# A five-layer decoder step on one core: another order and queue for the first loads of the scan, the first sines of cross attention behind the last scan, its output weights in eight pieces

## The chip, the core and the metric

The kernel runs on one core of one Trainium2 chip. A core has TensorE (PE: matmuls; PEld is its weight load), VectorE (DVE), ScalarE (ACT), GpSimd (POOL) and SyncE (SP). Loads and stores are issued from SP's and ACT's queues (and a few indirect ones from POOL's) and are moved by the core's 16 DMA engines. The metric is the device time of one execution in microseconds (us), as the median of several runs.

## The reference

Input `x` is 16 sequences of 128 tokens with 512 features. Two decoder layers follow one another; after each block the input is added and a layernorm taken. What matters here are the first two blocks.

The first is a state-space scan. For each token, `dt = softplus(x Wdt + b)` (512 values) and `B`, `C` (16 values each) come from products with `x`. With 16 states per feature the recurrence over the 128 tokens is

```
h = exp(dt * A) * h + (dt * x) * B
y = sum over the 16 states of h * C
```

and `y` goes through an output product with a bias.

The second is cross attention. Queries (16 heads of 128) come from `x`, keys and values (4 heads of 128) from 128 context tokens and the 128 tokens of `x`. Queries and keys are divided by their root mean square, weighted, and turned by rotary angles `position * inv_freq`, which needs the sine and cosine of 64 angles per token. Softmax over 256 keys, the values, and an output product (2048 by 512) follow. The rest (a ternary feed-forward, causal attention, a second cross attention, and a mixture of experts) is not touched.

## The kernel before, in words

Five stages run one after another. The work is cut into 16 blocks of 128 tokens, one per sequence.

The scan (`stage_ssm`) takes two blocks at a time and 16 states for each pair: 128 units. For a unit u, ACT forms the decays (`decays`, four exponentials), POOL the products `dBx` (`terms`), DVE runs the recurrence (`scan`), DVE or POOL multiplies by `C`, and PE adds the result into PSUM by transposes (`add`). SP loads `B` and `C` of unit u+4 (`widths_in`); POOL forms `dBx` of u+2. Between the units, PE also computes keys and values of the context for both attention blocks (`keys_values`), which are stored to DRAM. In this loop each instruction is pinned to the order in which the program writes it. `dBx` has four rooms, the copies `y` and `yT` of the output have three.

Ahead of the loop stand the first loads: the projection weights `xpw` and the first `xT` on SP, the step weights `dtw` (1 MB) on ACT, biases (`xpb`, three copies each of `dtb` and `outb`), `A_log`, and the weights `wk`, `wv` of the second cross attention (2 MB) on SP, then two context blocks. POOL makes each bias row into three bf16 parts (lines 156 to 164), then forms the four step sums (`step_sum`).

After the loop, a layernorm of the first two blocks, the last transposes, and the output product of the last pair (`output`, `output_sum`) close the stage. Then `load_output_weights` asks for the 4 MB of cross attention's output weights in two loads, into rooms of a pool of five: the rooms come free when the products that read them are done.

Cross attention (`stage_xattn`) loads the norm weights, positions and frequencies, forms with `SinTables` the sines and cosines of a group of four blocks (some 20 DVE instructions and two ACT ones), and multiplies them by the norm weights on POOL (`tables`). `project` then makes keys and queries of a block in steps: a load of the context's keys (`raw`), products on PE, the rotary step on DVE (`rope`), transposes on PE. Attention itself runs as a pipeline of 128 units, with `project` of the next block beside it. `clear_rows` issues some 100 DRAM clears of 388 KB for a later stage from SP's queue, one per step. Outside the scan's loop a scheduler orders each engine's instructions by its own estimate of when they become ready; `keep_in_program_order` holds one behind what is already written for its engine.

A tile's room is reused in turn: an instruction that writes a tile waits for the readers of the tile that had the room before.

Of the kernel before, what the change touches and what calls it, by code (L numbers as in the profile page):

```python
# [107 lines left out]
def stage_ssm(k):  # L108
# [9 lines left out]
    with ExitStack() as ctx:  # L118
# [20 lines left out]
        def load_x(p):  # L139
            xT = wk.tile([P, KC, TQ], F32, tag="xT", name="xT", bufs=1)  # L140
            nc.sync.dma_start(xT, a["xT"][:, p * TQ : (p + 1) * TQ].rearrange("(c p) t -> p c t", p=P))
            return xT

        nc.sync.dma_start(xpw, a["xpwT"].rearrange("(c p) e -> p c e", p=P))
        xT0 = load_x(0)
        nc.scalar.dma_start(dtw, a["dtwT"].rearrange("(c p) e -> p c e", p=P))
        nc.sync.dma_start(xpb, a["xpb"].unsqueeze(1))
        wholes = []
        for i, n in enumerate(("dtb", "outb")):
            whole = wk.tile([65, D], F32, tag="BC", name="whole", bufs=6)  # L150
            nc.gpsimd.memset(whole, 0.0)
            for r in (0, 32, 64):
                nc.sync.dma_start(whole[r : r + 1], a[n].unsqueeze(0))
            wholes.append(whole)
        nc.sync.dma_start(alog, a["A_log"].rearrange("(c p) n -> p c n", p=P))
# [16 lines left out]
        for i, n in enumerate(("wk", "wv")):  # L172
            nc.sync.dma_start(kvw[:, i], a["x2_" + n + "T"].rearrange("(c p) e -> p c e", p=P))
# [55 lines left out]
        def sums_out(st, i):  # L229
            y = wk.tile([P, KC, P], F32, tag="y", name="yT", bufs=3)  # L230
            q.nc.scalar.copy(y, st.py[i])
            st.yT[i] = y
# [6 lines left out]
        def turned_out(st, i):  # L239
            y = st.y[i] = wk.tile([P, KC, P], F32, tag="y", name="y", bufs=3)  # L240
            q.nc.scalar.copy(y, st.pt[i])
# [72 lines left out]
        def terms(u):  # L314
            st, n = units[u]
            dBx = st.dBx[n] = wk.tile([P, KC, TQ], F32, tag="dBx", name="dBx", bufs=4)
# [43 lines left out]
        nc.scalar.dma_start(outw, a["outwT"].rearrange("(c p) e -> p c e", p=P))  # L360
# [8 lines left out]
        for u, (st, n) in enumerate(units):  # L369
# [9 lines left out]
            if u >= 6:  # L379
                next(pieces, None)  # L380
            if n in (8, 9):
                i = n - 8
                q.nc.sync.dma_start(k.x[p * BQ + i], a["x"][p * BQ + i])
# [52 lines left out]
        q.nc.vector = nc.vector  # L436
        layernorm(k, k.x[0:2], k.x[0:2], keep=tc.keep_in_program_order)
        q.nc = nc
        if kv.out:
            keys_values_out()  # L440
# [9 lines left out]
    load_output_weights(k)  # L450


class SinTables:
# [4 lines left out]
    def __init__(self, k, pool, wk):  # L458
        nc, a = k.nc, k.args
        self.k, self.wk = k, wk  # L460
        pos = pool.tile([P, 2, NB], I32, name="pos")
        nc.sync.dma_start(pos, a["posT"].rearrange("s p b -> p s b"))
        self.invf = pool.tile([P, self.HF], F32, name="invf")
        nc.sync.dma_start(self.invf, a["inv_freq"].partition_broadcast(P))
        self.posf = pool.tile([P, 2, NB], F32, name="posf")
        nc.vector.tensor_copy(self.posf, pos)

    def group(self, g):
        nc, wk, HF, BG = self.k.nc, self.wk, self.HF, self.BG
# [7 lines left out]
        ang = wk.tile([P, N], F32, tag="m1", name="ang", bufs=4)  # L477
        r = wk.tile([P, N], F32, tag="m2", name="ang_r")
        sin = wk.tile([P, 2, BG, HF], F32, tag="sin", name="sin", bufs=1)
        cos = wk.tile([P, 2, BG, HF], F32, tag="cos", name="cos", bufs=1)  # L480
        for s in range(2):
            nc.vector.tensor_tensor(
# [3 lines left out]
            )  # L486
        for turns in (4096.0, 1.0):
            nc.vector.tensor_scalar(r, ang, 1.0 / (2 * PI * turns), MAGIC, ALU.mult, ALU.add)
            nc.vector.tensor_scalar(r, r, MAGIC, None, ALU.subtract)
            for c in parts:  # L490
                nc.vector.scalar_tensor_tensor(ang, r, -c * turns, ang, ALU.mult, ALU.add)
        lim = 3.1415925
        nc.vector.tensor_scalar(r, ang, lim, -lim, ALU.min, ALU.max)
        nc.scalar.activation(sin.rearrange("p s b f -> p (s b f)"), r, AF.Sin)

        r = wk.tile([P, N], F32, tag="m2", name="ang_r2")
        nc.vector.tensor_scalar(ang, ang, PI / 2, None, ALU.add)
        nc.vector.tensor_scalar(r, ang, PI, -2 * PI, ALU.is_gt, ALU.mult)
        nc.vector.tensor_tensor(r, r, ang, ALU.add)
        nc.vector.tensor_scalar(r, r, lim, -lim, ALU.min, ALU.max)  # L500
# [34 lines left out]
def load_output_weights(k):  # L535
    nc, a = k.nc, k.args
    k.wo = [k.wslot().rearrange("p (h e) -> p h e", h=8) for _ in range(2)]
    for i in range(2):
        nc.sync.dma_start(k.wo[i], a["xa_woT"][i * 1024 : (i + 1) * 1024].rearrange("(h p) e -> p h e", p=P))
# [20 lines left out]
def stage_xattn(k):  # L560
# [9 lines left out]
    with ExitStack() as ctx:  # L570
# [8 lines left out]
        w2 = []  # L579
        for name in ("q_norm_w", "k_norm_w"):  # L580
            w = cst.tile([P, HD], F32, name=f"w_{name}")
            nc.sync.dma_start(w, a[name].partition_broadcast(P))
            ws = cst.tile([P, HD], F32, name=f"ws_{name}")
            nc.vector.tensor_scalar(ws[:, 0:64], w[:, 64:128], -1.0, None, ALU.mult)
            nc.vector.tensor_copy(ws[:, 64:128], w[:, 0:64])
            w2.append((w, ws))
        sincos = SinTables(k, cst, wk)
        trig = {}
# [32 lines left out]
        def angles(g):  # L621
            trig[g] = sincos.group(g)
            yield

        def norm_inputs(p):
            xs = k.x[2 * p : 2 * p + 2]
            layernorm(k, xs, xs)
# [168 lines left out]
        running = [clear_rows(k, cst)]  # L796
# [1255 lines left out]
```

## Time and profile before

| what | value |
|---|---|
| runs | 3062.74, 3057.76, 3058.74 us |
| median | 3058.74 us |
| the profiled execution | 3050.86 us, span 3049.1 us |
| mean granted clock of TensorE | 0.991 |
| PE busy | 2925.1 us (96%) |
| DVE, ACT, POOL busy | 1891.8, 1355.2, 1491.1 us |
| first scan begins | 32.46 us |
| last scan ends | 507.2 us |
| first roped query turned on PE | 560.79 us |

A row of the timeline has start and duration in us, the engine, the line in the kernel, the operation, what it writes and reads, its shapes, and in brackets how long the engine was idle before it and what ended that. Several equal instructions are merged (x8). A row of SPq or ACTq is the issue of a transfer, not the transfer. Line 66 stands for every pinned instruction, so those are told apart by their tiles. The median of the runs lies 7.9 us above the profiled execution.

### The profile page before, as it was taken

How to read it: one execution, taken by the hardware profiler on the slowest of the kernel's cores; microseconds unless marked ns; L12 is line 12 of the kernel's file. 1: busy time of each engine (PE TensorE's matmuls, PEld its weight loads, DVE VectorE, ACT ScalarE, POOL GpSimd, SP SyncE). 2: the span in 40 equal slices, each digit the busy share in tenths (PEclk: the TensorE clock that was granted, in tenths of full speed). 3: DMA queues.
4: the chain of work that ended last, by engine and by line, in shares of the span. 5: the costliest groups of instructions: out<-in, count | busy, mean ns of one | idle time of the engine just before them, and what ended most of it. 6: DMA issues, size and time to landing. Idle time of an engine off the chain costs nothing.

```text
span 3049.1 us, 40643 instructions
## 1 busy us (share of the span) xinstructions
PE 2925.1 (96%) x13720; PEld 1832.3 (60%) x13744; DVE 1891.8 (62%) x4221; ACT 1355.2 (44%) x3315; POOL 1491.1 (49%) x1274
## 2 busy tenths in 40 slices
PE   7999999799999999999999989999999999999998
PEld 6666665455555555555787656666566666666665
DVE  5989997766666666655898797666643322242224
ACT  5777775333333343336444797655533322222221
POOL 7999995433333433331333574246535553333331
PEclk9999999899999999999999999999999999999999
DMA  6654444780000000004100200134356665554541
GB/s 189 205 140 123 125 128 140 251 290 11 11 8 11 11 8 15 8 26 149 35 1 1 70 1 2 60 110 163 126 188 236 225 226 168 164 192 165 163 149 60
DMA packets 170978, 331.59 MB, mean 109 GB/s; under 512 B 21966, under 2 KB 79822, under 8 KB 169228
## 3 DMA queue, kind: packets, MB, share of 16 engines
q1 hardware_dynamic: 127948, 222.01, 23.6%
q0 software_dynamic: 19200, 64.18, 6.2%
q10 hardware_dynamic: 23616, 42.74, 3.7%
q8 instruction: 111, 1.82, 0.2%
q14 instruction: 103, 0.84, 0.1%
HBM read 244.57 MB, written 137.43 MB: 125 GB/s over the span
## 4 chain that ended last, share of the span: by engine, by line
PE 67%; DVE 13%; ACT 2%; POOL 2%; issue 1%; DMA 1%; SPq 0%; ACTq 0%; DVEq 0%; POOLq 0%
PE y L1799 8%; PE pu L1782 7%; PE pg L1782 7%; PE pq L645 7%; PE po L765 6%; PE po L977 4%; PE ao L754 3%; PE sc L714 2%; PE pkv L66 2%; PE pt L508 2%; PE pg L957 2%; PE pw L1451 2%; PE pu L957 2%; PE ptx L508 1%; PE ps L1366 1%
## 5 line engine op out<-in xcount | busy, mean ns | idle before, releaser
L734 POOL TENSOR_TENSOR pr<-pr,sm 128x512 f32<-128x512 f32 x128 | 135.4, 1058 | 352.7 <-DVE sm L733 274.1
L66 POOL TENSOR_TENSOR dBx<-dtx,BC 128x1024 f32<-128x1024 f32 x126 | 298.4, 2390 | 0.6
L1782 PE MATMUL pg<-gu,xgT 128*128 128x352 f32 x784 | 296.5, 460 | 1.4 <-ACT act L1785 1.4
L1782 PE MATMUL pu<-gu,xgT 128*128 128x352 f32 x784 | 296.1, 459 | 0.0
L727 ACT ACTIVATE pr<-sc,mx,sf 128x256 f32<-128x256 f32 x256 | 142.2, 560 | 324.5 <-DVE mx L720 262.5
L1786 DVE SCALAR_TENSOR_TENSOR act<-pu,row,act 128x352 f32<-128x352 f32 x98 | 57.1, 582 | 358.2 <-PE pu L1782 353.1
L1799 PE MATMUL y<-dn,aT 128*128 128x512 f32 x588 | 268.4, 593 | 0.0
L1827 POOL TENSOR_TENSOR x<-got,x 128x512 f32<-128x512 f32 x120 | 151.6, 1269 | 222.3 <-DMA got<-results,gidx 221.8
L66 ACT ACTIVATE h<-dt,negA 128x254 f32<-128x254 f32 x508 | 242.2, 477 | 16.9
L765 PE MATMUL po<-w,aT 128*128 128x512 f32 x512 | 234.8, 597 | 2.5 <-DVE aT L759 2.5
L645 PE MATMUL pq<-w,xT 128*128 128x512 f32 x512 | 232.2, 596 | 1.3 <-ACT v L680 0.7
L1820 POOL DMA_INDIRECT got<-results,gidx x120 | 115.8, 965 | 230.7 <-DMA results<-yo 170.6
L66 DVE TENSOR_TENSOR_SCAN h<-h,dBx 128x1024 f32<-128x1024 f32 x80 | 183.2, 2290 | 34.4 <-ACT h L66 24.8
L1782 PEld LDWEIGHTS pu<-gu,xgT 128*128 128x128 f32 x784 | 149.0, 190 | 82.6 <-DVE act L1786 0.2
L1785 ACT ACTIVATE act<-pg 128x352 f32<-128x352 f32 x98 | 45.5, 464 | 304.3 <-PE pg L1782 269.4
L1782 PEld LDWEIGHTS pg<-gu,xgT 128*128 128x128 f32 x784 | 141.4, 190 | 64.7 <-ACT act L1785 1.9
L616 POOL TENSOR_TENSOR m<-m,m 128x512 f32<-128x512 f32 x96 | 121.4, 1265 | 111.8 <-DVE m L611 111.6
L66 PE MATMUL pkv<-w,cT 128*128 128x512 f32 x384 | 171.5, 593 | 1.1 <-ACT y L66 1.1
L1811 DVE COPY yo<-y 128x512 f32<-128x512 f32 x90 | 62.2, 691 | 165.6 <-PE y L1799 148.3
L1799 PEld LDWEIGHTS y<-dn,aT 128*128 128x128 f32 x588 | 104.2, 190 | 100.7 <-issue 94.1
L1774 ACT COPY xgT<-ptx 128x512 f32<-128x512 f32 x98 | 57.4, 586 | 234.5 <-PE ptx L508 228.9
L967 POOL TENSOR_TENSOR lo<-sg,hi 128x512 fp32r<-128x512 f32 x64 | 84.2, 1317 | 153.8 <-ACT hi L966 153.7
(402 smaller groups left out, 6770.3 us busy)
## 6 DMA issues: line engine op xcount, KB each, us to landing
bucket<-zeros SPq DMA_DIRECT2D x96, 388.0 KB, 8.0
row<-bucket SPq DMA_DIRECT2D x90, 388.0 KB, 3.7
BC<-bcd SPq DMA_DIRECT2D x128, 256.0 KB, 5.2
results<-yo ACTq DMA_DIRECT2D x90, 256.0 KB, 3.4
gu<-in_moe_guT SPq DMA_DIRECT2D x16, 1408.0 KB, 7.9
x_k<-kv ACTq DMA_DIRECT2D x32, 256.0 KB, 3.8
x_v<-kv ACTq DMA_DIRECT2D x32, 256.0 KB, 5.3
v<-x_v SPq DMA_DIRECT2D x32, 256.0 KB, 2.7
```

Of the source, the lines that this page charges most:

```text
L66: return self.tc.keep_in_program_order(call(*args, **kw))
L616: nc.gpsimd.tensor_tensor(m1, m1, m2, ALU.add)
L645: nc.tensor.matmul(ps, src[:, c], w[c], start=c == 0, stop=c == KC - 1)
L727: nc.scalar.activation(pr[:, j], st.sc[g, i][:, j], AF.Exp, scale=st.sf[:, h : h + 1], bias=st.mx[g, i][:, j : j + 1], accum_out=sm[:, j : ...
L734: nc.gpsimd.tensor_tensor(pr, pr, sm.unsqueeze(2).to_broadcast([P, 2, 2 * P]), ALU.mult)
L765: nc.tensor.matmul(st.po, aT[:, j], k.wo[h // 8][:, h % 8], start=h == 0, stop=h == G * J - 1)
L957: nc.tensor.matmul(p[:, e], w[:, c, at : at + P], sn.qT[:, :, c], start=c == 0, stop=c == KC - 1)
L977: nc.tensor.matmul(sn.po[i], part[:, e, i * P : (i + 1) * P], k.fd[hc // 8][:, hc % 8], start=hc == 0 and part is parts[0], stop=hc == 15 ...
L1782: nc.tensor.matmul(ps, u.xT[:, c], gu[:, c, lo : lo + I], start=c == 0, stop=c == KC - 1)
L1799: self.nc.tensor.matmul(u.y, u.aT[:, c], u.w[1][:, c], start=c == 0, stop=c == 2)
L1820: nc.gpsimd.indirect_dma_start(out=got[:, :], out_offset=None, in_=k.results[h][g][0:end, :], in_offset=bass.IndirectOffsetOnAxis(ap=self. ...
L1827: nc.gpsimd.tensor_tensor(k.x[b], got, k.x[b], ALU.add)
```

## The change

Four things change.

First, the loads at the start. The order on SP is written out and kept: `xpw`, `xT`, the three copies of `dtb`, `xpb`, `A_log`, and `outb` last (the scheduler puts the two context blocks ahead of `outb`). `dtw` comes in two halves on ACT. `wk` and `wv` move from SP's queue to ACT's, and the scan's output weights `outw` are kept behind the first keys on ACT.

Second, rooms: `dBx` has three instead of four, `y` and `yT` two instead of three. A new pool `head` holds the norm weights, positions and first sine tables through both stages.

Third, the head of cross attention. The four small loads are issued at unit 30 of the scan (`Head`), and the first group of angles is formed after the last scan, in two rooms of the tag `hs` that the scan no longer needs. These DVE instructions are kept in program order behind the layernorm, which is itself kept now; the same holds for the layernorms of later input blocks (`norm_inputs`).

Fourth, the output weights come in eight pieces of 512 KB, issued one per step of attention beginning with the third; the scheduler puts five of them ahead of the first `raw`.

```diff
-        xT0 = load_x(0)
-        nc.scalar.dma_start(dtw, a["dtwT"].rearrange("(c p) e -> p c e", p=P))
-        nc.sync.dma_start(xpb, a["xpb"].unsqueeze(1))
...
+        wholes = [wk.tile([65, D], F32, tag="BC", name="whole", bufs=6) for _ in range(2)]
+        def load_row(i):
+            for r in (0, 32, 64):
+                keep(nc.sync.dma_start(wholes[i][r : r + 1], a[("dtb", "outb")[i]].unsqueeze(0)))
+        for whole in wholes:
             nc.gpsimd.memset(whole, 0.0)
...
+        keep(nc.sync.dma_start(xT0, a["xT"][:, 0:TQ].rearrange("(c p) t -> p c t", p=P)))
+        load_row(0)
+        keep(nc.sync.dma_start(xpb, a["xpb"].unsqueeze(1)))
+        keep(nc.sync.dma_start(alog, a["A_log"].rearrange("(c p) n -> p c n", p=P)))
+        load_row(1)
+        for h in range(2):
+            es = slice(2 * h * P, (2 * h + 2) * P)
+            nc.scalar.dma_start(dtw[:, :, es], a["dtwT"][:, es].rearrange("(c p) e -> p c e", p=P))
...
-            nc.sync.dma_start(kvw[:, i], a["x2_" + n + "T"].rearrange("(c p) e -> p c e", p=P))
+            keep(nc.scalar.dma_start(kvw[:, i], a["x2_" + n + "T"].rearrange("(c p) e -> p c e", p=P)))
...
-            y = wk.tile([P, KC, P], F32, tag="y", name="yT", bufs=3)
+            y = wk.tile([P, KC, P], F32, tag="y", name="yT", bufs=2)
...
-            dBx = st.dBx[n] = wk.tile([P, KC, TQ], F32, tag="dBx", name="dBx", bufs=4)
+            dBx = st.dBx[n] = wk.tile([P, KC, TQ], F32, tag="dBx", name="dBx", bufs=3)
...
-        nc.scalar.dma_start(outw, a["outwT"].rearrange("(c p) e -> p c e", p=P))
+        keep(nc.scalar.dma_start(outw, a["outwT"].rearrange("(c p) e -> p c e", p=P)))
...
+            if u == 30:
+                k.head = Head(k, q.nc.sync)
...
-        q.nc.vector = nc.vector
-        layernorm(k, k.x[0:2], k.x[0:2], keep=tc.keep_in_program_order)
         q.nc = nc
+        layernorm(k, k.x[0:2], k.x[0:2], keep=keep)
+        room = [wk.tile([P, KC, TQ], F32, tag="hs", name="room") for _ in range(2)]
+        k.head.fill(keep)
+        k.head.trig = k.head.sines.group(
+            0, lambda what: {"ang": room[0][:, 0:2], "ang_r": room[1][:, 0:2], "ang_r2": room[1][:, 2:4]}[what]
+            .rearrange("p c t -> p (c t)") if what in ("ang", "ang_r", "ang_r2") else k.head.out[what], keep,
+        )
...
-    load_output_weights(k)
+class Head:
+    HD = 128
+    def __init__(self, k, sync):
+        a, pool = k.args, k.head_pool
+        self.k, self.raw, self.w2 = k, [], []
+        for name in ("q_norm_w", "k_norm_w"):
+            w = pool.tile([P, self.HD], F32, name=f"w_{name}")
+            sync.dma_start(w, a[name].partition_broadcast(P))
+            self.w2.append((w, pool.tile([P, self.HD], F32, name=f"ws_{name}")))
+        self.sines = SinTables(k, pool, sync)
+        self.out = {n: pool.tile([P, 2, SinTables.BG, SinTables.HF], F32, name=f"{n}0") for n in ("sin", "cos")}
+    def fill(self, keep):
+        vector = self.k.nc.vector
+        for w, ws in self.w2:
+            keep(vector.tensor_scalar(ws[:, 0:64], w[:, 64:128], -1.0, None, ALU.mult))
+            keep(vector.tensor_copy(ws[:, 64:128], w[:, 0:64]))
+        keep(vector.tensor_copy(self.sines.posf, self.sines.pos))
...
-def load_output_weights(k):
+def output_weights(k):
     nc, a = k.nc, k.args
     k.wo = [k.wslot().rearrange("p (h e) -> p h e", h=8) for _ in range(2)]
-    for i in range(2):
-        nc.sync.dma_start(k.wo[i], a["xa_woT"][i * 1024 : (i + 1) * 1024].rearrange("(h p) e -> p h e", p=P))
+    yield
+    yield
+    for n in range(8):
+        hs = slice(2 * (n % 4), 2 * (n % 4) + 2)
+        nc.sync.dma_start(k.wo[n // 4][:, hs], a["xa_woT"][n * 256 : (n + 1) * 256].rearrange("(h p) e -> p h e", p=P))
+        yield
...
-            layernorm(k, xs, xs)
+            layernorm(k, xs, xs, keep=tc.keep_in_program_order)
...
-        running = [clear_rows(k, cst)]
+        running = [output_weights(k), clear_rows(k, cst)]
...
-            if t == -12 or r == 0 and b > 0 and b < NB and b % 4 == 0:
-                running.append(angles(max(b, 0) // 4))
+            if r == 0 and b > 0 and b < NB and b % 4 == 0:
+                running.append(angles(b // 4))
```

The instructions of the first sines are the same 20 or so as before; the tables of the later groups stay where they were.

## The prediction

> **What bounds the kernel now.** I read the page's slices first, then the busy time by stretch, the waits, and the rows in order of time at the two places that the change touches.
>
> ```profile
> PE   7999999799999999999999989999999999999998
> POOL 7999995433333433331333574246535553333331
> ```
>
> A slice is 76.2 us. TensorE is full nearly everywhere, so a gain must be found where it is not: slice 0 (the start) and slice 7 (533 to 610, the way from the scan into cross attention). POOL is full through the scan. The busy time by stretch around slice 7 (PE, PEld, DVE, ACT, POOL, then clock and DMA):
>
> ```profile
> 508.00:527.00 19.00, 17.11 (x61) 8.64 (x60) 11.40 (x54) 3.97 (x7) 0.19 (x1) 1.00 0.37 137
> 527.00:541.00 14.00, 10.54 (x24) 4.10 (x22) 4.66 (x15) 3.45 (x5) 0.00 (x0) 1.00 0.75 239
> 541.00:560.00 19.00, 5.84 (x15) 3.13 (x16) 13.16 (x34) 1.39 (x3) 11.22 (x15) 0.55 0.96 317
> 560.00:600.00 40.00, 37.55 (x131) 20.24 (x130) 28.67 (x73) 16.29 (x38) 19.30 (x21) 1.00 0.81 280
> ```
>
> From 541 to 560 PE works 5.8 of 19 us, at a mean clock of 0.55, while VectorE is at 13.2. The waits from 500 to 600 (us, times, longest):
>
> ```profile
> POOL tk0s L595 <- ACT sin L494: 20.0, 1, 20.0
> PE pt L508 <- POOL m L677: 17.5, 4, 15.7
> DVE ws_q_norm_w L584 <- DMA raw<-x_k: 9.4, 1, 9.4
> ```
>
> One PE wait is 15.7 us; its cause is two steps back. The rows in order of time:
>
> ```profile
> 505.05 21.25 SPq L539 DMA_DIRECT2D w<-in_xa_woT  x2
> 526.67 0.34 SPq L582 DMA_DIRECT2D w_q_norm_w<-in_q_norm_w  x1
> 528.86 0.86 SPq L634 DMA_DIRECT2D raw<-x_k  x1
> ...
> 536.24 0.20 DVE L584 TENSOR_SCALAR ws_q_norm_w<-w_q_norm_w 128x64 f32<-128x64 f32 x1 [9.39 <-DMA raw<-x_k]
> 548.34 0.63 ACT L501 ACTIVATE cos<-ang_r 128x512 f32<-128x512 f32 x1 [1.91 <-DVE ang_r L500]
> 553.94 1.11 PE L508 MATMUL pt<-ident,m 128*128 128x128 f32 x4 [15.73 <-POOL m L677]
> 560.79 0.60 PE L508 MATMUL pt<-ident,m 128*128 128x128 f32 x4
> ```
>
> SP issues the first 2 MB of output weights at 505.05 and is held until 525.93 for the second (a room that PE still reads). Behind it stand the norm weights, positions and `raw`, which land at 536.3 to 536.9 because the second 2 MB go ahead of them. Only then do the sines start: 12.1 us on VectorE and ScalarE (536.24 to 548.34), then tables, the roped keys, and PE at 553.94. The start:
>
> ```profile
> 11.03 3.59 PE L182 MATMUL pb<-xT,xpw 128*32 128x256 f32 x8 [11.03 <-DMA alog<-in_A_log]
> 16.76 0.61 POOL L159 CAST rows_outb<-whole 65x512 bf16<-65x512 f32 x1 [0.46 <-DMA whole<-in_outb]
> 32.46 2.30 DVE L66 TENSOR_TENSOR_SCAN h<-h,dBx 128x1024 f32<-128x1024 f32 x1 [5.37 <-POOL dBx L317]
> ```
>
> Despite its label the first wait is for `xT`, landed at 10.90.
>
> **The change, part by part.**
>
> *A. Start.* Between 3 and 10 us the trace's DMA packets take 46 to 49 ns per 1 KB and 84 to 91 ns per 2 KB, and the two queues go about packet for packet (8 to 9 us: 121 of `xT` against 124 of `outw`). Without `outw` there, `xT` shares only with the rest of `dtw`: by 5.5 us some 0.85 of 1.05 MB are moved, so 0.4 MB together, then 0.3 MB alone, at 0.35 MB per us: 7.6, and 0.7 for the landing: 8.3 instead of 10.9. PE then runs pb (3.6) and the steps' matmuls (14.55 to 22.78, 8.2) to 20.1. POOL is what ends late: one bias row takes it 5.04 us (11.25 to 16.29; again 16.76 to 21.80). The first row's load lands behind `xT`, near 8.7, and is done at 13.7; the second now stands behind two context blocks. These are issued at 8.3, and from 10.9 their 512 B packets (27 ns) alternate with `wk` on ACT's queue (92 ns): 35 packets an engine, 4.1 us, to 15.0, landed 15.9, row done 20.95. Then POOL's four step sums (24.48 to 30.08, 5.6) and one product (2.39): scan at 28.95 against 32.46, **-3.5**. The other paths are ahead of it: the widths' store is now behind an ACT step that waits for PE, near 17.2, plus 5.7 and 4.5 as before for store and load makes 27.4, 0.9 late at worst; `outw` comes after and is first used a scan step-group later. Bounds: -1 if the context blocks take as long as before (8.4 us from issue to landing) and the widths are late too; -4.5 if POOL's second row were free. I take -3.5, worked from the nearest rows (packets of the same sizes).
>
> The Trainium skill, "DMA: Bandwidth & Descriptors", section "Rules for kernel authors", says that a transfer moved to another issuing engine runs on the same 16 DMA engines and saves only issue time. By that alone, moving two weight loads to ACT is worth their two issues (0.39 us each), and the sum below would be some 2.7 us smaller; the packet rows agree on the sharing, and add that a load's order and its neighbour on the other queue matter.
>
> *B. Scan.* With three `dBx` rooms the product of unit u waits for the scan of u-3. Rows of POOL and DVE set side by side: in all 125 cases the product begins later than that scan's end, by 0.50 us at the least (187.02 after 186.52), 2.6 at the median. So 0; but POOL has no gap before any product, so if this cover went, the wait would go straight into the loop. Four head loads (0.34+0.42+0.70+0.53 us of SP's issue) stand among BC loads issued four units (15 us) ahead: 0. Two `y` rooms instead of three: each copy follows the transposes that free its room anyway: 0.
>
> *C. Tail.* VectorE now runs, in this order: the layernorm, pinned (2 x 0.9 of statistics, 11 small steps at 0.2, 2 x 0.5: 5.0), 5 fills (0.6), 2 products (0.8), 12 sine steps (0.46 for scalar steps, 0.72 for dependent three-operand ones: 6.7), one add (0.4), and only then the first output sum. From 508.5 that is 522.0 against 521.46; PE's second output product, which waits for it, moves by **+0.6** (0 to 1.5). The two layernorms that ran here early are gone from this stretch. The rest (0.4+0.7+0.4) ends at 524.4, the cosine at 525.1, before ScalarE's copy of `xT` (526.06, now behind it on ACT): 1.5 us of cover; every us beyond delays the keys by one.
>
> *D. Into cross attention.* SP is still held: the order of the changed kernel has five quarter-pieces ahead of `raw`, and the fifth waits for the room as the second half did, 526.5 with C. But 0.5 MB instead of 2 MB goes ahead, and no head loads. 1.9 us from issue to first packet (525.93 to about 527.8), 256 packets at 180 per us (1.4), 128 of `raw` (0.7), 0.8 to land: 531.3. POOL's tables (four at 0.46 from 526.5) are done by 528.4. Then VectorE: the context keys' rope at its contended price (1.39+2x0.68+0.6=3.3; "m<-raw" has a median of 1385 ns), the own keys' 1.9, the root's 11 x 0.2: 538.7. POOL scales both (1.04 each), PE turns them at 539.8 and 540.8 where it did at 553.94 and 556.98; then one query product (3.44) whole, which before was half done. First roped query: key copies 1.2, rope 1.3, POOL add 1.27: 545.3 against 560.79. That is -15.5 with C, **-16.1** without. PE's only idle stretches are then about 1 us, so the half clock of 541.5 to 558.5 should not come. Bounds: `raw` as late as before gives -10; -18 if its rope is not contended. SP's later order puts the next `raw` behind six bucket clears and two weight pieces: landing near 549 (1.2 us a clear), wanted at 554; 5 us of cover.
>
> *E. Layernorms.* They are now pinned, so two move from the tail into attention, 4 us of VectorE each, next to a PE with 2.4 us idle in 40. VectorE has 11 idle us there. 0 to +4; I take **+1**, nearer to the hidden end.
>
> Sum: -3.5 + 0 + 0.6 - 16.1 + 1 = **-18.0 us**. It is made on the profiled execution, 3050.9 us (span 3049.1), 7.9 below the median of the runs, 3058.74. Same difference on the median: **3040.7**.
>
> **Rivals.**
> 1. Start gives little (-1), the rest holds: 3043. For it: POOL's row chain of 2 x 5.04 us stays, and its second load is later in the queue.
> 2. The change does half of what it says: SP's block is still there, so `raw` lands at 536.9 as before. D loses 5.6, and PE idles over 3.3 us, after which the clock halved twice in this trace (idle from 22.8, half at 26.05; idle from 538.2, half at 541.5), 1.5 us more: -10.9, 3048. Against it: a quarter of the bytes ahead.
> 3. Slower: POOL waits for scans. The point from which it decides is 24 us over 125 products, 0.19 us each on average, to end 0.2% above; at 0.5 us each it costs 62 and ends near 3103, at 0.25 near 3072. It needs a scan that falls back on POOL by more than the 0.5 to 2.6 us of cover, which no row shows.
> 4. More: A at -4.5, D at -18: 3038, or 3036 with E hidden and the tail at 0.
>
> **How the numbers follow.** Chances: forecast 0.56, first rival 0.14, second 0.13, third 0.06, fourth 0.08, something not seen (another stage's order shifted, within 0.2%) 0.03. A measurement here tells a change from none at about 0.2%, 6 us. Faster: forecast, first, second and fourth less 0.04 for ends that fall within 6 us: 0.87; same 0.07; slower 0.06. The range goes from the fourth rival less the 5 us that the runs shown lie apart (3057.8 to 3062.7), 3031, to the second plus the same, 3053; that leaves out rival 3, the unseen case and the outer ends of the others.
>
> **What would show it.** Right: `xT` landed by 9, first scan near 29; last scan about 3.5 us earlier; no DVE sine rows between the output sums and the first rope except the last three; no PE wait over 3 us before the first roped key; clock 1.0 throughout that stretch. Wrong: a gap before `dBx` on POOL, ScalarE's `xT` copy behind a late cosine, `raw` landed ten us after the scan's last output product, a PE wait for `mx` or `qT` near 570.

## The result and the profile after

The changed kernel takes 3035.45 us (median of six runs, 3031.15 to 3037.68); six runs of the kernel before on the same chip have a median of 3058.25 (3053.82 to 3063.67). The ratio is 0.9918 with a 95% interval of 0.9907 to 0.9929: 22.8 us less in the medians, which is under 1% and clear of the scatter. The profiled execution takes 3033.7 us with a span of 3031.8, which is 17.3 less than the span before. Those two figures differ, and the table below says where.

The page's slices of the changed kernel, for TensorE and POOL (76 us each):

```profile
PE   8999999999999999999999999999999999999998
POOL 8999996534334334332333663356435553333331
```

The 7 of slice 7 in TensorE's row has become a 9. The busy time by stretch of the changed kernel, for the four stretches that the prediction shows of before (PE, PEld, DVE, ACT, POOL, then clock, DMA share, GB/s):

```profile
508.00:527.00 19.00, 16.51 (x59) 8.30 (x58) 13.41 (x37) 6.44 (x10) 2.53 (x7) 1.00 0.31 115
527.00:541.00 14.00, 12.43 (x35) 5.45 (x34) 9.88 (x25) 2.35 (x4) 6.71 (x10) 1.00 0.84 245
541.00:560.00 19.00, 18.74 (x62) 9.48 (x61) 13.13 (x31) 6.76 (x11) 8.39 (x9) 1.00 1.01 361
560.00:600.00 40.00, 36.81 (x134) 20.57 (x133) 35.32 (x103) 17.94 (x50) 23.03 (x25) 1.00 0.67 224
```

From 541 to 560 TensorE now works 18.74 of 19 us where it worked 5.84, and at the full clock where the mean was 0.55. The rows in order of time of the changed kernel show why:

```profile
502.80 21.62 SPq L571 DMA_DIRECT2D w<-in_xa_woT  x5
521.82 0.63 ACT L529 ACTIVATE cos<-room 128x512 f32<-128x512 f32 x1 [1.95 <-DVE room L528]
524.67 0.34 SPq L665 DMA_DIRECT2D raw<-x_k  x1
528.50 0.69 DVE L640 TENSOR_TENSOR m<-raw,tk0c 128x512 f32<-128x512 f32 x1 [3.53 <-DMA raw<-x_k]
537.02 0.65 PE L536 MATMUL pt<-ident,m 128*128 128x128 f32 x4 [1.22 <-POOL m L708]
```

SP is held as before, to 524.06, with the fifth piece of the weights. But the cosine is done at 522.45, before the raw keys are even issued, and these are in VectorE's hands at 528.50 (ScalarE reads them first, at 528.21). TensorE turns the first roped keys at 537.02, 16.9 us earlier than before, after a wait of 1.22 us in place of 15.73. The start, from the rows of the same kernel:

```profile
7.76 3.59 PE L184 MATMUL pb<-xT,xpw 128*32 128x256 f32 x8 [7.76 <-DMA xT<-in_xT]
14.56 0.61 POOL L161 CAST rows_outb<-whole 65x512 bf16<-65x512 f32 x1 [1.92 <-DMA whole<-in_outb]
24.58 1.27 POOL L228 TENSOR_TENSOR dt<-dt,sp_v 128x512 f32<-128x512 f32 x1 [1.49 <-DVE sp_v L221]
29.66 2.30 DVE L66 TENSOR_TENSOR_SCAN h<-h,dBx 128x1024 f32<-128x1024 f32 x1 [5.22 <-POOL dBx L319]
```

`xT` is there at 7.76 (10.90 before), and the first scan begins at 29.66 (32.46). POOL's second bias row begins 2.2 us earlier than before and no longer ends last: POOL now waits 1.49 us for VectorE's step of the softplus.

Where the time went is read best from distances between the same instructions, since each stage's end shifts all that follows. The table gives, for every kernel of this study, the profiled execution's start of the first scan, end of the last scan, time from there to the first output product of cross attention (`po<-w,aT`), from the first such product to the last, and from the first transpose of the next stage's queries (`ptq`) to the first transpose of the routed rows (`ptx`). All are in us, each worked out from the trace's own start and end times.

| kernel | first scan | last scan ends | into attention | attention | ptq to ptx | span |
|---|---|---|---|---|---|---|
| before | 32.46 | 507.20 | 104.87 | 832.41 | 716.24 | 3049.1 |
| b_rooms | 32.83 | 508.35 | 104.79 | 829.64 | 718.88 | 3050.0 |
| b_norm | 31.37 | 506.55 | 105.91 | 823.93 | 723.91 | 3049.3 |
| changed | 29.66 | 504.95 | 89.93 | 824.02 | 724.76 | 3031.8 |
| u_again | 29.01 | 506.93 | 90.06 | 825.22 | 722.51 | 3033.5 |
| u_norm | 27.97 | 505.43 | 90.73 | 829.82 | 724.37 | 3040.4 |
| u_sines | 28.73 | 509.14 | 95.77 | 823.39 | 723.40 | 3040.6 |
| u_wo | 27.98 | 506.59 | 92.75 | 823.38 | 723.58 | 3035.4 |
| u_both | 29.27 | 506.08 | 93.95 | 824.21 | 724.57 | 3037.6 |
| late_wo | 28.49 | 505.73 | 89.52 | 826.14 | 718.61 | 3028.1 |
| u_start | 32.15 | 507.16 | 90.12 | 823.73 | 716.10 | 3026.9 |
| dbx2 | 29.09 | 520.16 | 89.91 | 826.30 | 715.81 | 3040.6 |
| psum_u | 29.81 | 496.17 | 90.13 | 825.85 | 721.27 | 3022.6 |
| psum_u2 | 28.66 | 494.50 | 90.18 | 823.33 | 715.65 | 3013.0 |

From before to changed: -2.25 by the last scan, -14.94 on the way into attention, -8.39 in attention, +8.52 between `ptq` and `ptx`, and -0.2 in the rest: -17.3, the difference of the spans. No edit touches the stretch from `ptq` to `ptx`, and over the fourteen kernels it takes 715.7 to 724.8 in no relation to what was edited. It goes with the chip instead, where the chip is on record: 715.7 for psum_u2 and 715.8 to 718.9 for late_wo, u_start, dbx2 and b_rooms, on two chips on which the kernel before has medians of 3054.6 and 3053.5; 721.3 to 724.6 for u_again, u_both and psum_u and 723.4 to 724.4 for b_norm, u_norm, u_sines and u_wo, on two chips on which it has 3059.1 and 3060.2. For the two profiles of this section no chip is on record; that the one of before (3050.86 us, below all six of its runs) comes from a chip of the first kind is a guess. So the pair of profiles holds a short one before and a long one after; without that stretch this pair gives -25.8. With means over the kernels that share a state of the edit, it is -1.4 (last scan: 507.37 over before, b_rooms, b_norm; 505.95 over changed, u_again, u_norm, u_wo, u_both, late_wo), -14.9, and -6.1 in attention (830.6 over before, b_rooms, u_norm; 824.5 over the eleven that pin the layernorms), -22.4 in all, against -22.8 in the medians.

### The profile page after: what moved, and what is told of

Same layout as the page of the kernel before. It is cut to its first block, busy times and chain, and to the rows that moved or that the text cites. A ratio compares the mean times of both kernels' runs of the same rounds, so it can differ in the third digit from the quotient of the medians.

```text
span 3031.8 us, 40699 instructions
## 1 busy us (share of the span) xinstructions
PE 2927.2 (97%) x13744; PEld 1830.9 (60%) x13744; DVE 1920.5 (63%) x4221; ACT 1356.5 (45%) x3315; POOL 1490.4 (49%) x1274
## 4 chain that ended last, share of the span: by engine, by line
PE 67%; DVE 13%; ACT 3%; POOL 1%; issue 1%; DMA 1%; SPq 0%; another core or an unknown queue 0%; DVEq 0%; ACTq 0%; POOLq 0%
PE y L1830 8%; PE pu L1813 7%; PE pg L1813 7%; PE pq L676 7%; PE po L796 6%; PE po L1008 4%; PE ao L785 3%; PE sc L745 3%; PE pt L536 2%; PE pg L988 2%; PE pu L988 2%; PE pT L773 1%; PE ptx L536 1%; PE pkv L66 1%; PE pw L1482 1%
## 5 line engine op out<-in xcount | busy, mean ns | idle before, releaser
L66 ACT ACTIVATE h<-dt,negA 128x254 f32<-128x254 f32 x508 | 242.2, 477 | 16.9
```

What stands on the lines that cost most here:

```text
L66: return self.tc.keep_in_program_order(call(*args, **kw))
```

## The experiments

Each ratio is to runs of the kernel before on the same chip, with its 95% interval. The chips differ (medians of before from 3053 to 3060), so ratios are compared, not times, but for kernels that ran on one chip; a difference of two ratios is uncertain by some 0.0018 (two half widths of about 0.0013, added in squares), 5.5 us.

### The pinned layernorms, alone and undone

The theory after the result: in the kernel before, each pair of query blocks has one wait of TensorE of about 1.2 us at a place where the unpinned input layernorm stood among the steps of a softmax, and the pins removed it. The prediction's step E said the opposite, a cost of 1 us. `b_norm` is the kernel before with the pin alone:

```diff
-            layernorm(k, xs, xs)
+            layernorm(k, xs, xs, keep=tc.keep_in_program_order)
```

> The kernel before, with one thing of the change alone: the input layernorms pinned in program order. Step E of the prediction: +1 us (0 to +4), about 3059. The theory from the two traces: the five PE waits of 1.2 us between 735 and 1183 go, -5 to -6 us, about 3053; nothing moves in the start or in the scan. The two layernorms that ran in the scan's tail go from there, which the tail does not feel: sines waited for a load, not for VectorE.

`u_norm` is the changed kernel without it:

```diff
-            layernorm(k, xs, xs, keep=tc.keep_in_program_order)
+            layernorm(k, xs, xs)
```

> The changed kernel, with the input layernorms again left to the scheduler and not pinned. The prediction's step E (two layernorms pushed into attention cost VectorE time beside PE): without the pins it gains 1 us, so about 3034.5, and no new PE stall appears. The theory formed from the two traces (the unpinned input layernorms were placed between two halves of another step, and each time PE waited 1.21 to 1.24 us for ScalarE's pTs: at 735.7, 846.8, 958.6, 1070.0 and 1182.0 before, nowhere after): these stalls come back, five of them, so it loses 5 to 6 us, about 3041; and in the tail two layernorms go ahead of the sines, so the sines' end and the keys move later by up to 5 us more, about 3046 at most.

Measured: b_norm 0.9974 (0.9965 to 0.9983), 8 us less than before; u_norm 0.9946 (0.9933 to 0.9959) against 0.9918, 8.6 us more than the changed kernel. TensorE's waits from 580 to 1375 (us in total, times, longest), first of the kernel before, then of b_norm, of the changed kernel and of u_norm:

```profile
PE pt L508 <- ACT pTs L745: 6.1, 5, 1.2
PE pt L508 <- POOL m L677: 3.4, 5, 1.3
```

```profile
PE pt L508 <- POOL m L677: 4.0, 5, 1.3
PE sc L714 <- ACT pr L727: 1.0, 1, 1.0
```

```profile
PE pt L536 <- POOL m L708: 2.4, 3, 0.8
PE po L796 <- DVE aT L790: 1.9, 1, 1.9
PE pT L773 <- DVE pTs L778: 1.5, 1, 1.5
PE sc L745 <- ACT pr L758: 1.0, 1, 1.0
```

```profile
PE pt L536 <- ACT pTs L776: 6.1, 5, 1.2
PE pt L536 <- POOL m L708: 1.9, 3, 0.6
```

The first line of before and the first of u_norm are the same five waits; the two pinned kernels do not have them. That the pins remove them is shown in both directions. What in them holds ScalarE's copy back is only argued: in the kernel before, VectorE's rows from 727.5 to 729.7 alternate between steps of the layernorm and steps of the keys' root and the softmax, and the copy `pTs` that TensorE waits for at 735.68 comes at the end of that chain. The medians give more than the five waits (8 against 6.1). Set side by side, the output products of b_norm gain on those of before about 1.4 us at each of the five places, 6.4 by 1387, and 2.1 more at the last ones, near 1400; of these 0.9 are one shorter wait (`po<-w,aT` for `aT`, 1.6 instead of 2.5), and the rest is open. u_norm does not lose them again there.

### The way into attention, part by part

Three kernels undo parts of it. `u_sines` leaves the early loads of positions and norm weights but forms the fills and the first sines after the scan, unpinned, as before:

```diff
-        k.head.fill(keep)
-        k.head.trig = k.head.sines.group(0, ...)
...
-        trig = {0: k.head.trig}
+        k.head.fill(lambda ins: ins)
+        trig = {}
...
+            if t == -12 or r == 0 and b > 0 and b < NB and b % 4 == 0:
+                running.append(angles(max(b, 0) // 4))
```

> The changed kernel, but the sign fills and the first group of sines are formed after the scan has ended, as before (loads of positions and norm weights still early, output weights still in pieces). Theory: some 6.7 us of VectorE and two ScalarE steps move between the landing of the raw keys (528 to 529) and the rope, so the first roped key leaves PE 5 to 9 us later, PE waits for it over 3 us and its clock halves for a while as it did at 541.5 before: +6 to +11 us, 3041 to 3046. Part of it comes back in the tail, where the second output product no longer waits (-0.4). Rival: the raw keys' landing alone sets the first roped key and the sines are formed while it is on its way, about 4 us of room: +2 or less, 3037.

`u_wo` leaves the sines in the tail and loads the output weights as before:

```diff
+    load_output_weights(k)          # at the end of the scan: two loads of 2 MB
...
-        running = [output_weights(k), clear_rows(k, cst)]
+        running = [clear_rows(k, cst)]
```

> The changed kernel, but the output weights are again two loads of 2 MB at the end of the scan's program, ahead of the raw keys; sines still early. Theory: SP is held for the second 2 MB until about 524, the raw keys queue behind all of it on the DMA engines and land near 535 instead of 528.5; the sines are done by then, so only the landing shifts: PE waits about 5 to 7 us longer for the first roped key: +5 to +9 us with the halved clock, 3040 to 3044. Rival (the sines alone had been the cause): +1 or less, 3035.

`u_both` has both of these edits.

> The changed kernel with both the sines formed after the scan and the output weights in two loads of 2 MB, so that of the way into attention only the early loads of positions and norm weights are left of the change. Theory A (what counts is when the first roped key is out: the sines' 12 us can run while the raw keys are on their way, 528 to 537, so the later of the two decides): no more than the larger of the two alone, +6 us against the changed kernel, and the early loads are worth the rest, about 6 us. Theory B (the two add): +8 to +10. Rival (the early loads are worth nothing, since in the kernel before they landed with the raw keys): +15, as before.

Measured: u_sines 0.9932 (0.9920 to 0.9944), u_wo 0.9906 (0.9891 to 0.9920), u_both 0.9934 (0.9920 to 0.9947); the changed kernel again, beside u_both on one chip, 0.9914 (0.9900 to 0.9928). In the column "into attention", which leaves the scan out, the three lose 5.8, 2.8 and 4.0 us against the changed kernel. In the medians u_sines loses 4.3 us, less than the 6 to 11 expected, but as expected its first roped key is turned 6.2 us later after the last scan and the clock halves (544.66 to 551.48). Rows of TensorE in u_wo:

```profile
534.49 3.70 PE L684 MATMUL pq<-w,xT 128*128 128x512 f32 x8 [0.68 <-ACT v L719]
540.56 5.39 PE L684 MATMUL pq<-w,xT 128*128 128x512 f32 x12 [2.37 <-DVE m L650]
546.75 0.66 PE L537 MATMUL pt<-ident,m 128*128 128x128 f32 x4 [0.80 <-POOL m L716]
```

And in u_both:

```profile
533.61 3.70 PE L679 MATMUL pq<-w,xT 128*128 128x512 f32 x8 [0.68 <-ACT v L714]
540.65 7.08 PE L679 MATMUL pq<-w,xT 128*128 128x512 f32 x12 [3.35 <-DVE m L645]
547.58 0.60 PE L531 MATMUL pt<-ident,m 128*128 128x128 f32 x4
```

In u_wo the raw keys are read 30.1 us after the last scan, as late as before (29.8; 23.3 in the changed kernel), and the first roped keys are turned 8 us later after the scan's end than in the changed kernel. Yet the stage loses 2.8 us, because TensorE does twelve matmuls of the next query product in front of the keys (they begin at 540.56, when VectorE has read the new key product out of PSUM) and has less of them to do behind. Its longest wait there is 2.4 us and the clock stays whole; in u_both a wait of 3.35 us is followed by 3.4 us at half clock (from 541.84). The runs show no loss from the 2 MB loads: 0.9906 against 0.9918 and 0.9914. The expected 5 to 9 us was wrong; the rival, that the sines alone matter, fits the runs within their scatter.

u_both stays at 93.95, below u_sines alone, so the parts don't add, as theory A has it: the sines run while the raw keys are under way (these are read 29.9 us after the last scan, and the cosine is done at 536.02, 0.1 us later). The kernel before takes 104.87 there. What is left of the change in u_both on this stretch is the early loads (with the fills, below), the pins and the rooms; the last two cost +1.0 and -0.1 in b_norm and b_rooms. The start's loads change nothing there (90.12 in u_start). So of the 14.9 us about 11 are put down, by difference, to having positions, frequencies and norm weights in SBUF before the raw keys are asked for. That part was not run by itself.

One thing in these two kernels was not expected. With the fills no longer pinned behind the scan, the scheduler put them into it, next to the loads that they read. VectorE's rows in u_both:

```profile
146.95 0.82 DVE L475 TENSOR_SCALAR ws_q_norm_w<-w_q_norm_w 128x64 f32<-128x64 f32 x1 [4.71 <-DMA w_q_norm_w<-in_q_norm_w]
147.69 2.28 DVE L66 TENSOR_TENSOR_SCAN h<-h,dBx 128x1024 f32<-128x1024 f32 x1
149.88 0.19 DVE L476 COPY ws_q_norm_w<-w_q_norm_w 128x64 f32<-128x64 f32 x1
150.00 2.38 DVE L475 TENSOR_SCALAR ws_k_norm_w<-w_k_norm_w 128x64 f32<-128x64 f32 x1
```

VectorE stands 4.71 us in the middle of the scan for a load, and a fill that takes 0.19 us in the tail of the changed kernel takes 2.38 there. The next scan, at 154.70, is 6.4 us behind the changed kernel's, of which u_both has made most good by its end and u_sines has not. So the times of u_sines hold some 3 us that are not the sines' (last scan at 509.14 against 505.95).

### The raw keys ahead of all weights

`late_wo` pins the weight pieces' issues, which puts the raw and value loads ahead of every one, and moves the last four pieces twelve steps later.

```diff
     for n in range(8):
+        if n == 4:
+            for _ in range(12):
+                yield
...
-        nc.sync.dma_start(k.wo[n // 4][:, hs], ...)
+        k.tc.keep_in_program_order(nc.sync.dma_start(k.wo[n // 4][:, hs], ...))
```

> The changed kernel, with the raw and value loads ahead of every piece of the output weights on SP, and the pieces of the second half twelve steps later. If SP's hold for the weights' room is what still delays the raw keys: they land 3 to 4 us earlier, but VectorE is busy with the tail's sines until about 524, so the first roped key comes 1 to 2.5 us earlier: -1 to -2.5 us, 3033. If the keys' room itself frees only with the tail: 0. If the first output product then waits for its weights: slower, by what PE waits there.

Measured: 0.9913 (0.9900 to 0.9927), no difference from the changed kernel. Rows of late_wo, and below them two of its waits (SP's for the raw keys, TensorE's for weights):

```profile
525.15 0.33 SPq L668 DMA_DIRECT2D raw<-x_k  x1
527.91 0.69 DVE L643 TENSOR_TENSOR m<-raw,tk0c 128x512 f32<-128x512 f32 x1 [2.17 <-POOL tqs L629]
```

```profile
SPq L668 <- PE po L249: 18.8, 1, 18.8
...
PE po L799 <- DMA w<-in_xa_woT: 1.9, 1, 1.9
```

With no weights in front, SP waits 18.8 us for the scan's last output product, and the raw keys go out at 525.15, 19.4 us after the last scan (19.7 in the changed kernel). So it is the end of the scan's tail that holds them now, not the weights. The first roped key is turned 30.7 us after the last scan instead of 32.1, the 1 to 2.5 us earlier that were expected; 0.4 us of it are left at the first output product, and the later pieces cost one wait of 1.9.

### The start alone

`u_start` is the changed kernel with the start's loads as before.

```diff
-        keep(nc.sync.dma_start(xT0, ...))      # first, rows and biases after it
...
+        nc.scalar.dma_start(dtw, ...)          # whole, beside xT
...
-            keep(nc.scalar.dma_start(kvw[:, i], ...))
+            nc.sync.dma_start(kvw[:, i], ...)
...
-        keep(nc.scalar.dma_start(outw, ...))
+        nc.scalar.dma_start(outw, ...)
```

> The changed kernel with the order and the queues of the start's loads as before. Theory from the two traces: the first scan starts at 32.4 to 32.6 instead of 29.7, and nothing behind it makes that good, since the scan is a chain: +2.8 us, 3038. The prediction's own figure: +3.5. Rival: the later first scan is made up inside the scan, which has room on VectorE: 0.

Measured: 0.9927 (0.9914 to 0.9941), 2.8 us above the changed kernel's 0.9918 and within the uncertainty of it. Its trace has the first scan at 32.15. Over all kernels the first scan begins at 32.20 with the old start (mean of four) and at 28.87 with the new (mean of ten), so the start is worth 3.3 us there. At the last scan 1.4 are left. Neither expectation holds as it was put: something in the scan takes about half back, and the last experiment shows one step that varies there.

### The rooms of the scan

`b_rooms` is the kernel before with three rooms for `dBx` and two for `y`:

```diff
-dBx = st.dBx[n] = wk.tile([P, KC, TQ], F32, tag="dBx", name="dBx", bufs=4)
+dBx = st.dBx[n] = wk.tile([P, KC, TQ], F32, tag="dBx", name="dBx", bufs=3)
```

> The kernel before with one thing of the change alone: three dBx rooms instead of four, and two y rooms instead of three. Theory (step B): 0 +- 2 us, no gap on POOL ahead of a product, since every product began 0.50 us or more after the scan that frees the third room. The third rival: products wait; at 0.19 us each +24 us, at 0.5 us +62.

`dbx2` takes one more room from the changed kernel (`bufs=2`), so that the cover is gone.

> The changed kernel with two dBx rooms instead of three, which takes the cover of step B away on purpose. In the trace of the changed kernel 71 of 126 products begin before the end of the scan two units back, by 136 us in all; moved along the measured steps of the two engines, with each product held for that scan and each scan for its product, the scan ends 26 to 42 us later. Theory (the wait goes straight into the loop, as the third rival has it): +26 to +42 us, 3061 to 3077. Rival (POOL has other work that it can do late, so the loop takes the wait up): under +10.

Measured: b_rooms 0.9998 (0.9988 to 1.0007), no effect; dbx2 0.9955 (0.9941 to 0.9969), 11 us more than the changed kernel. POOL's groups in the scan, of b_rooms and then of dbx2 (busy us, mean ns, then idle time in front and its releasers):

```profile
L66 POOL TENSOR_TENSOR dBx<-dtx,BC 128x1024 f32<-128x1024 f32 x126 | 298.6, 2394 | 1.1 <-DMA BC<-bcd 0.6
```

```profile
L66 POOL TENSOR_TENSOR dBx<-dtx,BC 128x1024 f32<-128x1024 f32 x126 | 302.3, 2408 | 41.3 <-DVE hs L66 25.0 <-DVE h L66 15.1
```

With three rooms no product waits for a scan. With two, POOL waits 41.3 us for scans, and the last scan ends 14 us later than the mean of the changed kernels, not 26 to 42. A part of the waits is taken back: the softplus step of the next experiment is shorter in dbx2 (21.8 us for 14 of them, 32.2 in u_again), where POOL pauses more often; that this is the reason was not tested.

### A step of VectorE that POOL holds

`u_again` is the changed kernel unaltered.

> The changed kernel once more, unaltered, on the chip of the other two of this group. Everything that the theory says of it has been measured: the ratio to the kernel before again 0.991 to 0.993, 19 to 27 us less. Its profiled execution is wanted for the scatter: the first scan between 28.0 and 29.7 as in the six executions that begin like it, the scan 475 to 479 long.

Measured: 0.9914 (0.9900 to 0.9928), span 3033.5, first scan at 29.01 and the scan 477.9 long, as expected. In the kernels so far, but for dbx2, groups of 16 scans take 60.5 or 60.6 us in most cases and 58.2 in a few, once the first two groups are over (and the third in u_both and u_sines). Set side by side, the two kinds differ in one instruction, `sp_v<-sp_u,sp_v` of `step_rest`. VectorE's rows in a long group of u_again, then POOL's over the same time:

```profile
236.09 1.23 DVE L66 TENSOR_TENSOR hC<-h,BC 128x1024 f32<-128x1024 f32 x1
237.23 4.21 DVE L66 SCALAR_TENSOR_TENSOR sp_v<-sp_u,sp_v 128x512 f32<-128x512 f32 x1
241.55 0.69 DVE L66 SCALAR_TENSOR_TENSOR sp_v<-pd,sp_v 128x512 f32<-128x512 f32 x1
```

```profile
236.23 4.67 POOL L66 TENSOR_TENSOR dBx<-dtx,BC 128x1024 f32<-128x1024 f32 x2
242.38 1.27 POOL L66 TENSOR_TENSOR dt<-dt,sp_v 128x512 f32<-128x512 f32 x1 [1.49 <-DVE sp_v L66]
```

POOL's two products end at 240.90, and VectorE's step, begun at 237.23, ends 0.54 later. Then POOL waits for it. In a short group the step gets in between the two products and takes 1.7 to 1.9. In all 14 cases of u_again the step ends 0.55 us after the end of a product, and in five of them that is the second product to end since the step began; the cases of 0.8 us began some 0.26 before such an end. Of the two steps, one reads both operands from SBUF (0.81 to 4.24 us) and the other one from PSUM (0.69 always). `psum_u` rewrites the two so that each reads one operand from PSUM; the value is the same up to rounding:

```diff
+        def step_max(st, h):
+            v, u = st.vu[h]
+            q.nc.vector.scalar_tensor_tensor(u, st.pd[h], 0.0, v, ALU.max, ALU.add)
+
         def step_one(st, h):
-            q.nc.scalar.activation(u, v, AF.Identity, bias=1.0)
+            q.nc.scalar.activation(st.pd[h], v, AF.Identity, bias=1.0)
...
-            q.nc.vector.scalar_tensor_tensor(v, u, 1.0, v, ALU.subtract, ALU.subtract)
-            q.nc.vector.scalar_tensor_tensor(v, st.pd[h], 0.0, v, ALU.max, ALU.subtract)
+            q.nc.vector.scalar_tensor_tensor(v, st.pd[h], 1.0, u, ALU.subtract, ALU.subtract)
...
-(st.dt[:, 2 * h : 2 * h + 2], st.vu[h][1], AF.Ln)
+(st.dt[:, 2 * h : 2 * h + 2], st.pd[h], AF.Ln)
...
-(st.dt[:, hs], st.dt[:, hs], st.vu[h][0], ALU.add)
+(st.dt[:, hs], st.dt[:, hs], st.vu[h][0], ALU.subtract)
...
+            if n in (5, 9) and nxt:
+                step_max(nxt, n // 9)
```

> The changed kernel with one step of the scan written in another order: of the two VectorE steps of the softplus, both read one operand from PSUM, where one read two from SBUF. In the executions so far that one takes 0.8 us when POOL is not multiplying and 4.2 us when POOL runs products back to back, five or six times in a scan, and a group of 16 scans then takes 60.6 us where it takes 58.2 when the step gets through (1.9 us). Theory (the step is held by POOL's products through its second SBUF operand): with one operand in PSUM it takes 0.7 us every time, and the scan is 5 or 6 x 2.35 us shorter: -12 to -14 us, last scan near 493. Rival (a step of three operands is held whatever it reads, or POOL becomes the bound as soon as VectorE is free): 0 to -3.

Measured: 0.9880 (0.9865 to 0.9895), 3023.25 us beside 3031.99 of u_again on the same chip, and 36 us less than the kernel before. VectorE's groups in the scan, of u_again and then of psum_u:

```profile
L66 DVE SCALAR_TENSOR_TENSOR sp_v<-sp_u,sp_v 128x512 f32<-128x512 f32 x14 | 32.2, 2302 | 0.0
L66 DVE SCALAR_TENSOR_TENSOR sp_v<-pd,sp_v 128x512 f32<-128x512 f32 x14 | 9.7, 692 | 1.5
```

```profile
L66 DVE SCALAR_TENSOR_TENSOR sp_u<-pd,sp_v 128x512 f32<-128x512 f32 x14 | 9.7, 692 | 17.3 <-ACT sp_v L66 17.3
L66 DVE SCALAR_TENSOR_TENSOR sp_v<-pd,sp_u 128x512 f32<-128x512 f32 x14 | 9.5, 680 | 0.0
```

The expectation misread the traces in two points: POOL is multiplying beside the cases of 0.8 us too, and the step is held four or five times in most kernels, not five or six. In psum_u the step takes 0.68 us all 14 times, each time with POOL busy from its start to its end, 22.7 us less in all; the scan is 466.4 long where u_again's is 477.9, and the last scan ends at 496.2 instead of 505.9 on the mean. The theory holds, the size is a little under what was expected: about 10 us on the mean (8.7 in the medians, 11.5 beside u_again, where five holds of 2.35 make 11.8) instead of 12 to 14. There is a new wait of 17.3 us in front of the first step, so the match with 11.8 may be chance. `psum_u2` was to take that wait away by placing `step_max` one unit later, in front of that unit's scan:

```diff
                 if n in (6, 10):
+                    step_max(nxt, n // 10)
                     step_one(nxt, n // 10)
...
-            if n in (5, 9) and nxt:
-                step_max(nxt, n // 9)
```

> The version with the softplus steps from PSUM, with the first of the two VectorE steps one unit later, ahead of that unit's scan. In the version before it, VectorE waits 17.3 us in 14 places (1.2 each) for ScalarE's exponential in front of this step. Theory (VectorE and POOL share the bound in the scan, and POOL waits 16 us for VectorE's scans): the wait goes, and 4 to 8 us of the scan with it, ratio 0.9855 to 0.9865. Rival (ScalarE's next step now waits for VectorE and delays the decays that the scans need: VectorE waits 24 us for them already): 0 or slower.

Measured: 0.9875 (0.9859 to 0.9892), no difference from psum_u. The wait is still 17.3 us: behind one scan and in front of the next is the same place on VectorE, so the edit moved nothing there, and neither its theory nor its rival was tested. It stands as a second measurement of the same version, the fastest of this study: 1.2% under the kernel before and 0.3 to 0.4% under the changed one.

## Why the prediction was right, and where it was not

The total was forecast as -18.0 us and 3040.7; measured are -22.8 in the medians and 3035.45, in the range and on the right side. By steps:

- **A, start, -3.5.** At the first scan -2.8 in the pair of profiles and -3.3 over all kernels: right in size. `xT` came earlier than worked out (7.76, not 8.3). The reason given for the end of the path, POOL with its two bias rows, was wrong: POOL is done with them at 19.96 and waits for VectorE at 24.58. And the step took for granted that the scan passes its whole gain on ("last scan about 3.5 us earlier"). At the last scan 1.4 are left on the mean. How often the softplus step is held (4.2 us four times in before, b_rooms and b_norm; four to five times in changed, u_again, u_norm, u_wo and late_wo, but three times in u_both) may cover part of that difference of 1.9; the rest stays open.
- **B, scan, 0.** Right, by b_rooms. The cover did shrink: the smallest distance from a scan's end to the product that takes its room was 0.50 us before and is 0.08 in the changed kernel. The third rival's mechanism is real, but its price was too high. It put the waits straight into the loop; with two rooms POOL waits 41 us and the scan grows by 14.
- **C, tail, +0.6.** Measured against the last scan's end, the second output product moves from 15.00 to 15.38 us: +0.4, and it waits for VectorE as said (1.15 us). The cosine was done before the copy of `xT`, as said.
- **D, into attention, -16.1.** With C the forecast was -15.5, worked out at the first roped query. Counted from the last scan's end that query is turned 16.5 us earlier (37.1 against 53.6), and 14.9 are left at the first output product. Set back by what the scan's end moved (2.25), the roped keys were turned at 539.3 where 539.8 was worked out, and the raw keys were read at 530.5 where 531.3 stood. No half clock, no wait of TensorE over 3 us: as said. What the working got wrong is the share of the parts. The second rival priced late raw keys at 5.6 us plus a halved clock; u_wo has the late raw keys, and they cost 2.8 on the stretch, no halved clock, and nothing that the runs can tell. TensorE has query products to do meanwhile; the kernel before does the next ones only behind the first turned keys (two at 554.84, five at 557.89). The larger part, about 11 us by difference, is that the loads of the sines no longer stand behind the weights.
- **E, pinned layernorms, +1 (0 to +4).** The sign was wrong. The pins gain: -6.1 us in attention over all kernels, -8 in b_norm. The step weighed VectorE's total time in two stretches and did not ask where in a pair of blocks the unpinned layernorm stood. The profile of before had the sign in one line that the working does not use, the five waits of TensorE of 1.2 us for `pTs`.

So -18.0 came out 4.4 us short of -22.4: E was wrong by 7.1, and A's loss within the scan, 2.1, and 0.6 in C and D went the other way. That the total came so close is in part luck: it holds a step of the wrong sign, and errors of 7.1 and 2.7 us that partly cancel.

## What to carry to other kernels

Where a stage's first result needs several loads, ask which of them stands last in its queue and what work could already run if only that one were early: here small loads of positions and norm weights were worth more than making the big ones smaller. A late result costs only what the engine behind it has no other work for, so look for that work before pricing the delay. And where a scheduler may place a step freely, read from the waits where it did place it: five waits of 1.2 us, and in two variants a load waited for in the middle of a scan, came from steps that were left unpinned.

## What the runs showed of the hardware that was not expected

A VectorE step of 512 elements that reads both operands from SBUF (`sp_v<-sp_u,sp_v`) took between 0.81 and 4.24 us beside POOL's products in u_again. All 14 ended about half a us after the end of a product, five of them after the second of two that ran back to back. With one operand in PSUM it took 0.68 us every time in psum_u, with POOL busy throughout. The Trainium skill, "SBUF — State Buffer", section "Who interferes with whom", says that a VectorE instruction with two SBUF inputs contends with a GpSimd instruction that reads SBUF, and calls the pair of ports that they share an exclusive lock, in which the second to issue waits for the first.

The step agrees with that, and psum_u is the test of it; why it let a second product pass in five cases is open. Another pair of SBUF operands fits too: in the changed kernel VectorE's `m<-raw,tk0c` took 0.69 us the one time that POOL was idle beside it and 1.38 to 1.64 the 15 times that POOL was busy, and there too it ended about half a us after the end of POOL's `m<-m,m`. Other rows do not fit: in the scan of the changed kernel all 128 scans (`h<-h,dBx` and `hs<-h,dBx`, two SBUF operands) took 2.27 to 2.30 us and the products `hC<-h,BC` on VectorE 1.22 to 1.23, while POOL was busy 96% of the time. So two operands in SBUF are not enough to be held; what sets the steps that are held apart from those was not found.
